# A message-passing layer on one core: the last split's loop re-ordered, one root for pair and finishing, filler products ahead of it

## The chip, the cores and the metric

The kernel runs on one core of one Trainium2 chip. The core has five engines with queues of their own: TensorE (PE in the profile; its weight loads are PEld), VectorE (DVE), ScalarE (ACT), GpSimd (POOL) and SyncE (SP, which here only starts transfers). They meet through semaphores. On-chip data lie in SBUF, and products land in the eight banks of PSUM. The metric is the device time of one execution, in microseconds (us); lower is better.

## The reference

```python
row, col = edge_index                                   # 100000 edges, 6250 nodes, D = 128
msg_in = concatenate([x[row], x[col], edge_attr], -1)   # 384 wide
h = msg_in @ W + b
mu, var = mean(h, -1), mean((h - mu)**2, -1)
h = (h - mu) * rsqrt(var + 1e-5) * gamma + beta
out = segment_sum(relu(h), row)                         # per source node
return layernorm(x + out)                               # no gain, no offset
```

Each edge takes a row of x for its source and one for its target, goes through one linear layer, a layer norm and a relu, and is summed into its source node. At the end each node is normalised once more.

## The kernel before

The linear layer is split by the three parts of its input. For the source part a table xa lies in SBUF, as three bf16 terms whose sum is the f32 value, for 50 blocks of 125 nodes. The target part and the edge part are computed edge by edge in the order in which the edges come (by target), and written to DRAM by an indirect transfer on POOL's queue (L561), sorted by block of the source. Each written row is 132 wide: 128 values and, in column D, the source's place in its block. The edges are worked off in six *splits*; each has its own sorted area, and while the products of one split are scattered, the blocks of the split before it are gathered and summed. The blocks are taken two at a time, as 25 *pairs* for each split.

What is done for one pair p of a split with k tiles of 128 edges a pair (k = 4 in the last split) are the methods of `Pair`:

- `load_pair` (L610): one transfer on SP's queue brings the pair's sorted rows into a tile hl (4 buffers).
- `ones` (L627): DVE compares column D with 0..127 and writes a one-hot, ohe, in f32 (4 buffers).
- `turn` and `turned` (L636, L647): PE transposes the one-hot into the bank tr (there is one), and ACT copies it out as bf16, ohn (2 buffers).
- `pick` (L656): PE adds, for each tile, the three terms of xa chosen by ohn onto hl. In the last split hl itself gets into the bank (of sel or hp) by a product with the identity, L665; in the other splits ACT copies it there (`seed`, L650).
- `square` (L675): ACT squares the k tiles with a running sum each (L680) and takes the root (L683).
- `root` and `scale` (L686, L691): DVE takes the reciprocal (L689), multiplies by it and cuts from below (L695), which gives msg (2 buffers).
- `sums` (L698): PE multiplies the one-hot with msg and sums over edges in the bank pa (there is one). `add` (L707): DVE adds pa to acc in SBUF (L712).

`Finish` does the last norm for the two blocks of a pair once the last split has been added: `begin` (L722) loads x for them on SP's queue and starts y on POOL (L728, L729; on DVE for the last pair); `stats` (L731) ends y and sums it on DVE; `root` (L740) squares on ACT (L745) and takes a root (L748); `norm` and `moved` (L750, L755) make the reciprocal (L753) and the shift (L758) on DVE; `end` (L761) multiplies and adds on POOL as two operations on 256 elements (L764, L765; by ACT, L768, for the last pair), and stores on SP's queue (L770).

PE, DVE, ACT and SP run in the order in which the program text issues the instructions; POOL's order is a scheduler's. Up to the last split, `work` (L876) issues the steps of all pairs of splits 0 to 4 from the table FLOW, in between the products of the edges. The last split has nothing of the edges beside it. Its order is `tail(i)` (L962), called once for each pair and six more times: it holds steps of pairs i+2 to i-1 and of finishings i-1 to i-5. Ahead of it, the last calls of `work` still issue steps of the last pairs of split 4, and `tail(-2)` and `tail(-1)` stand among them:

```python
    for p in range(2):
        load_pair(s, p)
    work(n_last - 8 - n_steps)
    tail(-2)
    work(n_last - 4 - n_steps)
    tail(-1)
    work(n_last - n_steps)
```

The first load of the last split waits for the last scatter of the edges to land, as its rows may be anywhere in the sorted area.

Of the kernel before, what the change touches and what calls it, by code (L numbers as in the profile page):

```python
# [8 lines left out]
F32 = mybir.dt.float32  # L9
# [7 lines left out]
P = 128  # L17
# [33 lines left out]
XG = 4  # L51
ROW = 132
# [29 lines left out]


def fast_path(ctx, tc, io, bad_d):
# [533 lines left out]
    class Pair:  # L618
# [8 lines left out]
        def ones(self):  # L627
# [4 lines left out]
            nc.vector.tensor_tensor(self.ohe[:, :k, :],  # L632
                                    self.hl[:, :k, D:D + 1].to_broadcast([P, k, P]),
                                    row_bc(iota_p, k), op=ALU.is_equal)
# [20 lines left out]

        def pick(self, g):  # L656


            j0, m = self.groups[g]
            if g in self.sel:  # L660
                sel = self.sel[g]
            else:
                name = "hp" if (g + self.p * len(self.groups)) % 2 else "sel"
                sel = psum.tile([P, PT, P], F32, name=name, bufs=BANKS[name])
                nc.tensor.matmul(sel[:, :m, :], ident, self.hl[:, j0:j0 + m, 0:D], start=True,  # L665
                                 stop=False, skip_group_check=True)
                self.sel[g] = sel
            for j in range(m):
                b = 2 * self.p + (j0 + j) % 2
                for i in range(3):  # L670
                    pe(nc.tensor.matmul(sel[:, j, :], self.ohn[:, j0 + j, :],  # L671
                                        xa[:, b, i * D:(i + 1) * D], start=False,
                                        stop=j == m - 1 and i == 2, skip_group_check=True))

# [41 lines left out]
    class Finish:  # L716
# [5 lines left out]
        def begin(self):  # L722
            fin, b0, n = late["fin"], self.b0, self.n
            xs = fin.tile([P, FN, D], F32, name="xs", bufs=3)
            nc.sync.dma_start(flat(xs), io["xblk"][:, b0 * D:(b0 + n) * D])
            self.y = fin.tile([P, FN, D], F32, name="y", bufs=6)
            engine = nc.gpsimd if b0 + n < NB else nc.vector
            engine.tensor_tensor(self.y, acc[:, b0:b0 + n, 0:D], row_bc(g2, n), op=ALU.mult)  # L728
            engine.tensor_tensor(self.y, self.y, xs, op=ALU.add)  # L729

        def stats(self):  # L731
            fin, y = late["fin"], self.y
            total = fin.tile([P, FN], F32, name="total", bufs=4)
            for j in range(self.n):
                nc.vector.scalar_tensor_tensor(y[:, j, :], beta_p, acc[:, self.b0 + j, D:D + 1],
                                               y[:, j, :], op0=ALU.mult, op1=ALU.add,
                                               accum_out=total[:, j:j + 1])
            self.total = total

        def root(self):  # L740
            fin = late["fin"]
            fsq = fin.tile([P, FN, D], F32, name="fsq")
            var = fin.tile([P, FN], F32, name="var")
            for j in range(self.n):
                nc.scalar.activation(fsq[:, j, :], self.y[:, j, :], AF.Square, scale=-float(D),  # L745
                                     bias=self.total[:, j:j + 1], accum_out=var[:, j:j + 1])
            self.std = fin.tile([P, FN], F32, name="fstd", bufs=3)
            nc.scalar.activation(self.std, var, AF.Sqrt, bias=eps, scale=1.0 / D ** 3)  # L748

        def norm(self):  # L750
            fin = late["fin"]
            self.rstd = fin.tile([P, FN], F32, name="frstd", bufs=3)
            nc.vector.reciprocal(self.rstd, self.std)  # L753

        def moved(self):  # L755
            fin = late["fin"]
            self.shift = fin.tile([P, FN], F32, name="shift", bufs=3)
            nc.vector.scalar_tensor_tensor(self.shift, self.total, -1.0 / D, self.rstd,  # L758
                                           op0=ALU.mult, op1=ALU.mult)

        def end(self):  # L761
            y, n = self.y, self.n
            if self.b0 + n < NB:
                nc.gpsimd.tensor_tensor(y, y, col_bc(self.rstd[:, :n], D), op=ALU.mult)  # L764
                nc.gpsimd.tensor_tensor(y, y, col_bc(self.shift[:, :n], D), op=ALU.add)  # L765
            else:
                for j in range(n):
                    nc.scalar.activation(y[:, j, :], y[:, j, :], AF.Identity,  # L768
                                         bias=self.shift[:, j:j + 1], scale=self.rstd[:, j:j + 1])
            nc.sync.dma_start(io["out"][:, self.b0 * D:(self.b0 + n) * D], flat(y))  # L770
# [183 lines left out]
    f = [Finish(2 * p, 2) for p in range(n)]  # L954

    def at(p):
        return 0 <= p < n

    first_g = range(len(x[0].groups) - 1)
    last_g = len(x[0].groups) - 1  # L960

    def tail(i):  # L962
        if at(i - 1):
            x[i - 1].root(last_g)
        if at(i + 2):
            x[i + 2].ones()
            if at(i + 4):
                load_pair(s, i + 4)
        if at(i - 1):
            x[i - 1].scale(last_g)  # L970
        if at(i):
            for g in first_g:
                x[i].pick(g)
                x[i].square(g)
            x[i].pick(last_g)
        if at(i - 4):
            f[i - 4].root()
        if at(i + 1):
            x[i + 1].turn()
            x[i + 1].turned()  # L980
        if at(i):
            x[i].square(last_g)
        if at(i - 5):
            f[i - 5].end()
        if at(i - 3):
            f[i - 3].stats()
        if at(i - 4):
            f[i - 4].norm()
        if at(i):
            for g in first_g:  # L990
                x[i].root(g)
        if at(i - 4):
            f[i - 4].moved()
        if at(i - 1):
            x[i - 1].sums()
        if at(i):
            for g in first_g:
                x[i].scale(g)
        if at(i - 1):
            x[i - 1].add()  # L1000
            f[i - 1].begin()


# [265 lines left out]
```

## Time and profile before

| | us |
|---|---|
| median of three runs | 1138.0 |
| lowest, highest | 1137.83, 1139.56 |
| the profiled execution | 1138.6 |
| its span, first to last instruction | 1136.7 |
| busy in the span: PE, DVE, POOL, ACT | 859.8, 882.7, 837.0, 735.6 |
| last scatter issued (start) | 1033.08 |
| first one-hot of the last split (start) | 1037.87 |
| last row of arithmetic (end) | 1129.76 |

The profile is of one execution. Its page gives busy times of the engines, the chain of work that ended last, and groups of instructions by line. The trace behind it can be asked for windows (busy time of each engine and the clock that TensorE was granted, as a share of full speed), for a timeline, and for the instructions of one line. Times in it count from the first instruction. A row of the timeline gives start, length, engine, line, operation, what it writes and reads, and in brackets how long its engine had been idle and what ended that.

POOL is 74% busy over the span, nearly all of it with the scatters, 782 of them at 986 ns each. The last split runs after the last of these, in the last tenth of the span.

### The profile page before, as it was taken

How to read it: one execution, taken by the hardware profiler on the slowest of the kernel's cores; microseconds unless marked ns; L12 is line 12 of the kernel's file. 1: busy time of each engine (PE TensorE's matmuls, PEld its weight loads, DVE VectorE, ACT ScalarE, POOL GpSimd, SP SyncE). 2: the span in 40 equal slices, each digit the busy share in tenths (PEclk: the TensorE clock that was granted, in tenths of full speed). 3: DMA queues.
4: the chain of work that ended last, by engine and by line, in shares of the span. 5: the costliest groups of instructions: out<-in, count | busy, mean ns of one | idle time of the engine just before them, and what ended most of it. 6: DMA issues, size and time to landing. Idle time of an engine off the chain costs nothing.

```text
span 1136.7 us, 27306 instructions
## 1 busy us (share of the span) xinstructions
PE 859.8 (76%) x8671; PEld 798.3 (70%) x8671; DVE 882.7 (78%) x2444; ACT 735.6 (65%) x3104; POOL 837.0 (74%) x899
## 2 busy tenths in 40 slices
PE   3657755445877878787778878898989899986994
PEld 2546644345877778686777877888988898975673
DVE  7987776326878777778677778988999987875996
ACT  1334332115666676576766777887988999994996
POOL 2777777777777777777777777777777777773786
PEclk9878786657989989899889999998999999998998
DMA  6799996438877756677777749776877677742562
GB/s 198 230 282 280 292 288 203 140 105 263 252 243 241 246 179 190 216 241 243 226 244 225 229 125 316 253 251 205 279 249 237 209 230 221 237 140 88 159 171 83
DMA packets 126674, 247.47 MB, mean 218 GB/s; under 512 B 47356, under 2 KB 61197, under 8 KB 126519
## 3 DMA queue, kind: packets, MB, share of 16 engines
q1 hardware_dynamic: 100356, 191.52, 56.2%
q0 software_dynamic: 25184, 53.31, 13.2%
q8 instruction: 70, 1.15, 0.4%
q10 hardware_dynamic: 978, 0.80, 0.3%
q14 instruction: 86, 0.70, 0.2%
HBM read 155.74 MB, written 89.80 MB: 216 GB/s over the span
## 4 chain that ended last, share of the span: by engine, by line
PE 29%; DMA 24%; DVE 24%; ACT 11%; issue 7%; POOL 2%; SPq 1%; ACTq 0%; POOLq 0%; DVEq 0%
DMA sorted<-hs,place_i 18%; PE pa L704 9%; DVE msg L695 7%; PE hp L531 7%; PE sel L671 6%; DMA db<-drel_d 4%; ACT sq L680 3%; DVE ohe L632 3%; DVE sc L391 3%; PE beside L428 2%; ACT sel L654 2%; POOL sorted L561 2%; ACT hs L543 2%; ACT ohn L648 2%; PE tr L644 2%
## 5 line engine op out<-in xcount | busy, mean ns | idle before, releaser
L561 POOL DMA_INDIRECT sorted<-hs,place_i x782 | 771.0, 986 | 240.9 <-issue 98.8
L704 PE MATMUL pa<-msg,ohe 128*128 128x130 f32 x1900 | 268.1, 292 | 23.3 <-DVE acc L712 15.3
L531 PE MATMUL hp<-w,eT 128*128 128x128 f32 x1564 | 248.2, 309 | 49.2 <-ACT hs L543 44.3
L543 ACT COPY hs<-hp 128x512 f32<-128x512 f32 x196 | 114.0, 582 | 258.7 <-DMA sorted<-hs,place_i 193.3
L671 PE MATMUL sel<-xa,ohn 128*128 128x128 bf16 x2706 | 198.7, 225 | 106.3 <-ACT sel L654 105.5
L671 PEld LDWEIGHTS <-ohn 128*128 128x128 bf16 x2850 | 182.9, 100 | 133.5 <-issue 112.6
L704 PEld LDWEIGHTS pa<-msg,ohe 128*128 128x128 f32 x1900 | 240.3, 201 | 34.3 <-DVE acc L712 18.7
L695 DVE SCALAR_TENSOR_TENSOR msg<-sel,rstd,cut 128x128 f32<-128x128 f32 x902 | 255.2, 345 | 8.0
L531 PEld LDWEIGHTS hp<-w,eT 128*128 128x128 f32 x1564 | 221.2, 218 | 54.6 <-ACT hs L543 48.8
L680 ACT ACTIVATE sq<-sel 128x128 f32<-128x128 f32 x902 | 238.1, 282 | 17.4 <-PE sel L671 16.7
L680 ACT ACTIVATION_READ_ACCUMULATOR sq<-sel 128x1 f32 x902 | 191.6, 212 | 0.0
L632 DVE TENSOR_TENSOR ohe<-hl,beside 128x1024 f32<-128x1024 f32 (+2 forms) x150 | 147.9, 986 | 37.4 <-DMA hl<-sorted 30.9
L654 ACT COPY sel<-hl 128x512 f32<-128x512 f32 (+1 forms) x225 | 127.9, 568 | 19.4 <-DVE msg L695 19.1
L648 ACT COPY ohn<-tr 128x1024 bf16<-128x1024 bf16 (+2 forms) x150 | 123.7, 825 | 18.4 <-PE tr L644 18.2
L689 DVE RECIPROCAL rstd<-std 128x4 f32<-128x4 f32 (+1 forms) x250 | 42.9, 172 | 84.7 <-ACT std L683 83.8
L519 DVE TENSOR_SCALAR ohd<-db,part_w 128x512 bf16<-128x512 bf16 x194 | 71.8, 370 | 46.7 <-DMA db<-drel_d 25.2
L644 PE MATMUL tr<-ident_h,ohe 128*128 128x128 bf16 x950 | 81.6, 226 | 10.5 <-issue 7.2
L535 PE MATMUL hp<-win,ohd 126*128 126x128 bf16 x782 | 83.3, 233 | 4.1 <-DVE ohd L519 3.5
L683 ACT ACTIVATE std<-ss,eps 128x4 f32<-128x4 f32 (+1 forms) x250 | 74.3, 297 | 8.1
L535 PEld LDWEIGHTS <-ohd 126*128 126x128 bf16 x782 | 66.9, 106 | 8.7 <-DVE ohd L519 3.7
L712 DVE TENSOR_TENSOR acc<-acc,pa 128x260 f32<-128x260 f32 x125 | 52.3, 418 | 26.4 <-PE pa L704 26.3
L644 PEld LDWEIGHTS <-ohe 128*128 128x128 bf16 x950 | 63.8, 102 | 11.8 <-issue 7.7
(159 smaller groups left out, 807.6 us busy)
## 6 DMA issues: line engine op xcount, KB each, us to landing
eT<-in_eT SPq DMA_DIRECT2D x96, 512.0 KB
hl<-sorted SPq DMA_DIRECT2D x75, 528.0 KB
db<-drel_d SPq DMA_DIRECT2D x96, 256.0 KB
sorted<-empty SPq DMA_DIRECT2D x100, 198.0 KB
hl<-sorted SPq DMA_DIRECT2D x50, 264.0 KB
sorted<-hs,place_i POOLq DMA_INDIRECT x782
hl<-sorted SPq DMA_DIRECT2D x25, 396.0 KB
sorted<-empty SPq DMA_DIRECT2D x50, 132.0 KB
```

The source lines that it names most:

```text
L531: pe(nc.tensor.matmul(hp[:, j, :], eT[:, at], w[:, 2, :], start=j == 0, stop=False, skip_group_check=True), 4)
L535: pe(nc.tensor.matmul(hp[:, j, :], oh[:3 * WN, at], win[:3 * WN, :], start=False, stop=j == m - 1, skip_group_check=True))
L543: nc.scalar.copy(hs[:, :m, 0:D], hp[:, :m, :])
L561: i = nc.gpsimd.indirect_dma_start(out=sorted_d[s][:, :], out_offset=bass.IndirectOffsetOnAxis(ap=place_i[:parts, t:t + 1], axis=0), in_=h ...
L632: nc.vector.tensor_tensor(self.ohe[:, :k, :], self.hl[:, :k, D:D + 1].to_broadcast([P, k, P]), row_bc(iota_p, k), op=ALU.is_equal)
L644: pe(nc.tensor.transpose(tr[:, j, :], half[:, j0 + j, 1::2], ident_h))
L648: nc.scalar.copy(self.ohn[:, :self.k, :], self.tr[:, :self.k, :])
L654: nc.scalar.copy(self.sel[g][:, :m, :], self.hl[:, j0:j0 + m, 0:D])
L671: pe(nc.tensor.matmul(sel[:, j, :], self.ohn[:, j0 + j, :], xa[:, b, i * D:(i + 1) * D], start=False, stop=j == m - 1 and i == 2, skip_gro ...
L680: nc.scalar.activation(sq[:, j, :], self.sel[g][:, j, :], AF.Square, accum_out=ss[:, j:j + 1])
L695: nc.vector.scalar_tensor_tensor(self.msg[:, j0 + j, 0:D], self.sel[g][:, j, :], rstd[:, j:j + 1], cut, op0=ALU.mult, op1=ALU.max)
L704: pe(nc.tensor.matmul(self.pa[:, h, :], self.ohe[:, j, :], self.msg[:, j, :], start=(j == h), stop=(j == k - 2 + h)), 4)
```

## The change

The steps of the last pairs of split 4 now all end before the first one-hot of the last split is issued. Four pairs are loaded ahead instead of two. Fourteen products of 128x512 ones, whose result nothing reads, are issued on PE between the old pairs' last sums and the new pairs' first product, all into the one bank tr. The order of `tail` is a new one, called for i from -1 to n+3. In it one tile of sums takes the squares of pair i (4 columns) and of finishing i-3 (2 columns), ACT takes one root of all six, and DVE one reciprocal; to fit the finishing's scale, the pair's squares are now of 128 times the value. The identity product of pair i+1 is issued a turn ahead (`begin_pick`), the sums of pair i-1 last in PE's turn. The add and the begin of the finishing move from one pair behind to two. x is loaded at i+1, three turns ahead of its use, into 5 buffers instead of 3. POOL ends a finishing by one fused multiply and add for each block, with scalars per partition; the last two are shared by ACT and DVE.

```diff
+WARM = 14
...
+        def begin_pick(self, by_pe):
+            m = self.k
+            name = "hp" if self.p % 2 else "sel"
+            sel = psum.tile([P, PT, P], F32, name=name, bufs=BANKS[name])
+            if by_pe:
+                nc.tensor.matmul(sel[:, :m, :], ident, self.hl[:, :m, 0:D], start=True,
+                                 stop=False, skip_group_check=True)
...
+        def squares(self, ss):
+            sq = late["blk"].tile([P, PT, P], F32, name="sq")
+            for j in range(self.k):
+                nc.scalar.activation(sq[:, j, :], self.sel[0][:, j, :], AF.Square,
+                                     scale=float(D), accum_out=ss[:, j:j + 1])
...
-            if self.b0 + n < NB:
-                nc.gpsimd.tensor_tensor(y, y, col_bc(self.rstd[:, :n], D), op=ALU.mult)
-                nc.gpsimd.tensor_tensor(y, y, col_bc(self.shift[:, :n], D), op=ALU.add)
...
+                    engine.tensor_scalar(y[:, j, :], y[:, j, :], self.rstd[:, j:j + 1],
+                                         self.shift[:, j:j + 1], op0=ALU.mult, op1=ALU.add)
...
+    def roots(i):
+        lo, hi = 0 if at(i) else kp, kp + FN if at(i - 3) else kp
+        if lo == hi:
+            return
+        std = late["blk"].tile([P, kp + FN], F32, name="tstd", bufs=2)
+        nc.scalar.activation(std[:, lo:hi], sums_of.pop(i)[:, lo:hi], AF.Sqrt, bias=eps,
+                             scale=1.0 / D ** 3)
+        rstd_of[i] = std, lo, hi
+
+    def reciprocals(i):
+        if i not in rstd_of:
+            return
+        std, lo, hi = rstd_of.pop(i)
+        rstd = late["blk"].tile([P, kp + FN], F32, name="trstd", bufs=4)
+        nc.vector.reciprocal(rstd[:, lo:hi], std[:, lo:hi])
+        if at(i):
+            x[i].rstd[0] = rstd
+        if at(i - 3):
+            f[i - 3].moved(rstd[:, kp:kp + FN])
 
     def tail(i):
+        if i == -1:
+            x[0].begin_pick(True)
+        if at(i):
+            x[i].pick(0)
+        if at(i + 1):
+            x[i + 1].turn()
+        reciprocals(i - 1)
+        if at(i - 2):
+            x[i - 2].add()
+            f[i - 2].begin(nc.gpsimd if i - 2 < n - 1 else nc.vector)
+        if at(i + 2):
+            ones_at(i + 2)
+            load_next()
+        if at(i - 1):
+            x[i - 1].scale(0)
+        if at(i + 1):
+            if i >= 0:
+                x[i + 1].begin_pick(True)
+            f[i + 1].load()
+        if at(i - 2):
+            f[i - 2].stats()
+        if at(i) or at(i - 3):
+            sums_of[i] = late["blk"].tile([P, kp + FN], F32, name="tsums", bufs=3)
+        if at(i - 3):
+            f[i - 3].square(sums_of[i][:, kp:])
+        if at(i):
+            x[i].squares(sums_of[i])
+        roots(i)
+        if at(i + 1):
+            x[i + 1].turned()
+        if at(i - 1):
+            x[i - 1].sums()
+        if at(i - 4):
+            f[i - 4].end([nc.gpsimd] if i - 4 < n - 2 else [nc.scalar, nc.vector])
+            f[i - 4].store()
...
-    for p in range(2):
-        load_pair(s, p)
-    work(n_last - 8 - n_steps)
-    tail(-2)
-    work(n_last - 4 - n_steps)
-    tail(-1)
-    work(n_last - n_steps)
+    for p in range(4):
+        load_next()
+    work(n_last + 1 - n_steps)
+    for p in range(WARM):
+        tr = psum.tile([P, PT, P], F32, name="tr", bufs=BANKS["tr"])
+        nc.tensor.matmul(flat(tr), ones_h, row_bc(ones_h, PT), start=True, stop=True)
     nc.vector.tensor_copy(beta_p, beta2)
-    for i in range(n + 6):
+    ones_at(0)
+    for i in range(-1, n + 4):
         tail(i)
```

The old `tail`, whose lines are left out of the diff, is printed above.

More of the change, by code (lines that the diff above doesn't have):

```diff
@@ L736, in stats, with square @@
                                                y[:, j, :], op0=ALU.mult, op1=ALU.add,
[L737 to L743, printed above, removed]
+                                               accum_out=self.total[:, j:j + 1])
+        def square(self, var):
+            fsq = late["fin"].tile([P, FN, D], F32, name="fsq")
             for j in range(self.n):
@@ L746, in root, with moved, end, store @@
                                      bias=self.total[:, j:j + 1], accum_out=var[:, j:j + 1])
[L747 to L758, printed above, removed]
+        def moved(self, rstd):
+            self.rstd = rstd
+            self.shift = late["fin"].tile([P, FN], F32, name="shift", bufs=3)
+            nc.vector.scalar_tensor_tensor(self.shift, self.total, -1.0 / D, rstd,
                                            op0=ALU.mult, op1=ALU.mult)
[L761 removed]
+        def end(self, engines):
             y, n = self.y, self.n
[L763 to L767 removed]
+            for j in range(n):
+                engine = engines[j % len(engines)]
+                if engine is nc.scalar:
                     nc.scalar.activation(y[:, j, :], y[:, j, :], AF.Identity,
                                          bias=self.shift[:, j:j + 1], scale=self.rstd[:, j:j + 1])
[L770 removed]
+                else:
+                    engine.tensor_scalar(y[:, j, :], y[:, j, :], self.rstd[:, j:j + 1],
+                                         self.shift[:, j:j + 1], op0=ALU.mult, op1=ALU.add)
+        def store(self):
+            nc.sync.dma_start(io["out"][:, self.b0 * D:(self.b0 + self.n) * D], flat(self.y))
     n_split = len(SPLITS)
```

90 lines of the change are left out of this document (34 added, 56 removed).

## Prediction

> **What bounds the kernel now.** I read the busy windows first, because the diff touches only the last split and the hand-over to it. The columns are the stretch, its length, then busy time (and instructions) of PE, PEld, DVE, ACT and POOL, the granted TensorE clock, the DMA share and GB/s.
>
> ```profile
> 1033.00:1033.50 0.50, 0.00 (x0) 0.00 (x0) 0.33 (x2) 0.00 (x0) 0.42 (x1) 0.88 0.37 127
> 1043.50:1044.00 0.50, 0.50 (x11) 0.50 (x9) 0.00 (x0) 0.00 (x0) 0.00 (x0) 0.88 0.00 0
> 1060.00:1080.00 20.00, 19.15 (x162) 14.17 (x163) 18.76 (x85) 18.73 (x97) 16.28 (x26) 1.00 0.63 170
> ```
>
> Two stages show. The two 0.88 rows are mixtures of 1.00 and 0.50, which puts a fall of the clock to half near 1033.4 and its rise near 1043.6. From 1060 on PE, DVE and ACT are each over 93% busy at full clock, so this stage is a loop among three full engines. The chain of waits (start, length, what) shows who holds whom, first across the hand-over, then over two pairs of the steady stage:
>
> ```profile
> 1035.24 2.61 DMA hl<-sorted
> 1037.87 0.69 DVE ohe L632
> 1038.56 0.35 DVE acc L712
> 1038.95 2.10 PE pa L704 x8
> ...
> 1057.05 0.59 ACT ohn L648
> ...
> 1059.22 0.57 DVE ohe L632
> 1059.79 0.27 DVE msg L695
> 1060.20 1.36 PE pa L704 x8
> 1061.56 0.86 PE sel L665 x2
> 1062.42 0.67 PE sel L671 x12
> 1063.09 0.24 PE tr L644 x4
> ```
>
> The hand-over waits for the first load of the last split until 1037.87. Only then, since L632 stands ahead of it on DVE, comes an old pair's add L712, which PE's old sums had been waiting for; and they run at half clock, 2.10 us against the 1.16 of the row at 1017.97 below. The first square of the last split starts at 1044.92. The second fence is one turn of 1063.35 - 1057.05 = 6.30 us for two pairs. Between the copy and the one-hots lie ACT's squares and root. In the turn PE alone gives 1.36 + 0.86 + 0.67 + 0.24 = 3.13 us a pair, with the sums paced by the scales, which come just ahead of them. From the timeline (start, length, engine, line):
>
> ```profile
> 1017.97 1.16 PE L704 MATMUL pa<-msg,ohe 128*128 128x130 f32 x8 [0.82 <-DVE acc L712]
> 1018.97 0.39 PE L644 MATMUL tr<-ident_h,ohe 128*128 128x128 bf16 x4
> 1019.19 0.83 PE L671 MATMUL sel<-xa,ohn 128*128 128x128 bf16 x12
> 1020.06 0.28 ACT L680 ACTIVATE sq<-sel 128x128 f32<-128x128 f32 x1
> 1021.24 0.30 ACT L683 ACTIVATE std<-ss,eps 128x4 f32<-128x4 f32 x1
> 1021.44 0.58 ACT L654 COPY sel<-hl 128x512 f32<-128x512 f32 x1
> 1044.44 0.59 ACT L648 COPY ohn<-tr 128x512 bf16<-128x512 bf16 x1 [2.34 <-PE tr L644]
> 1044.92 0.28 ACT L680 ACTIVATE sq<-sel 128x128 f32<-128x128 f32 x1
> 1045.15 0.83 PE L671 MATMUL hp<-xa,ohn 128*128 128x128 bf16 x12
> 1120.08 0.26 ACT L680 ACTIVATE sq<-sel 128x128 f32<-128x128 f32 x1
> 1128.88 0.88 ACT L768 ACTIVATE y<-y,shift,frstd 128x128 f32<-128x128 f32 x2 [0.71 <-DVE shift L758]
> ```
>
> So the 25 pairs take 1120.08 - 1044.92 = 75.16 us from first to last square (24 steps of 3.13), and the drain takes 1129.76 - 1120.08 = 9.68 us. These are the three terms of the sum: hand-over, step, drain. All before the hand-over stays as it is.
>
> **The change, part by part: the steady step.** One root and one reciprocal now serve a pair and the finishing three pairs behind it. That takes L748 from ACT and L753 from DVE; the squares of the finishing go ahead of those of the pair; the sums of pair i-1 go to the end of PE's turn, behind the next identity product (L665).
>
> ```profile
> L745 ACT ACTIVATE fsq<-y,total 128x128 f32<-128x128 f32 x50 | 19.3, 387 | 2.0 <-DVE y L735 2.0
> L748 ACT ACTIVATE fstd<-var,eps 128x2 f32<-128x2 f32 x25 | 7.4, 296 | 0.8
> L753 DVE RECIPROCAL frstd<-fstd 128x2 f32<-128x2 f32 x25 | 4.0, 160 | 0.9 <-ACT fstd L748 0.9
> L728 POOL TENSOR_TENSOR y<-acc,g 128x256 f32<-128x256 f32 x24 | 16.4, 685 | 18.9 <-DVE rstd L689 17.5 <-DVE acc L712 1.4
> L729 POOL TENSOR_TENSOR y<-y,xs 128x256 f32<-128x256 f32 x24 | 17.5, 728 | 5.3 <-DMA xs<-in_xblk 3.8
> L764 POOL TENSOR_TENSOR y<-y,frstd 128x256 f32<-128x256 f32 x24 | 14.7, 614 | 6.6 <-DVE frstd L753 6.4
> masks.py:199 POOL TENSOR_SCALAR_AFFINE_SELECT ident<-ident 128x128 f32<-128x128 f32 x1 | 0.3, 282 | 0.0
> ```
>
> What is then the longest loop? In after's order every ACT copy of a one-hot (ohn) releases its products, these the pair's squares, these the root, and the next copy stands behind the root. Its links, start to start: copy to products 1045.15 - 1044.44 = 0.71; products to squares 1020.06 - 1019.19 = 0.87; squares to root 1021.24 - 1020.06 = 1.18; root to the next copy 1021.44 - 1021.24 = 0.20. Sum 2.96 us, against 3.13 now. The engines' own queues must be shorter. ACT: copy 0.48 (1044.92 - 1044.44), finishing squares 2 x 0.39 = 0.78, then 1.18 and 0.20: 2.64. PE: 0.67 + 0.24 + 0.86, and sums no longer paced, 1.00 (1018.97 - 1017.97): 2.77. DVE: of its 18.76 us in 20, that is 2.93 a pair, 0.16 goes: 2.77. POOL: L728 and L729 1.41, plus two fused operations, plus about 0.08 between any two (1087.43 less 1086.74 + 0.61, below). The fused operation has no row. Its bounds are 0.28 (the one POOL operation of that shape with one tensor) and 0.61 (L764, two tensors and twice the elements); I take 0.33, nearer the first, as it has the same shape and one more scalar. POOL then needs 1.63 + 0.66 = 2.29. With 0.61 it needs 2.85, still under 2.96. The wait for xs (3.8 us in all on L729) goes too, but POOL is not on the path, so I count nothing; the cover is the 0.6 us by which POOL is shorter than the step.
>
> I take 2.96: 24 x 2.96 = 71.04, a gain of 4.12 us. Bounds: no gain, if PE stays the bound at 3.13; and 2.77, the longest queue, a gain of 8.7 us, which I hold for out of reach because the loop of links allows no overlap.
>
> The queues the steps pass: the hl load of pair i+5 now waits on SP for PE's identity product of pair i+1; behind it stand the xs load and the store of pair i-4. A load has three steps (8.9 us) to land where the first took 2.61, so this costs nothing. On DVE the finishing's sums (L735) wait for POOL's two operations on the add just made: 0.39 to reach the other engine (1038.95 - 1038.56), 1.41 and 0.08 give 1.88 us after the add's start, while add, one-hots and scales (1.13, the row at 1032.20 below) fill 0.35 + 0.57 + 1.13 = 2.05. That is tight: once POOL is late by more than this 0.17 and DVE's slack of 2.96 - 2.77 = 0.19 together, each further tenth costs 2.4 us over the split.
>
> DVE's shift (L758) is the other place where POOL reaches DVE:
>
> ```profile
> 1086.74 0.61 POOL L764 TENSOR_TENSOR y<-y,frstd 128x256 f32<-128x256 f32 x1 [0.38 <-DVE frstd L753]
> 1087.43 0.61 POOL L765 TENSOR_TENSOR y<-y,shift 128x256 f32<-128x256 f32 x1
> 1089.49 0.72 POOL L729 TENSOR_TENSOR y<-y,xs 128x256 f32<-128x256 f32 x1 [0.80 <-DMA xs<-in_xblk]
> 1089.72 0.51 DVE L758 SCALAR_TENSOR_TENSOR shift<-total,frstd 128x2 f32<-128x2 f32 x1
> ```
>
> The shift took 0.51 here and ended at 1090.23, when POOL's operation did. In the changed order it stands behind the joint reciprocal and may meet a fused operation, of 0.33 by my price, under the add's own wait for PE. I charge nothing. The Trainium skill (SBUF — State Buffer, Who interferes with whom) says that a VectorE instruction with two SBUF inputs is blocked for as long as a GpSimd instruction that reads SBUF runs. The trace agrees in this row, and the rule speaks against the change in that short POOL operations in a row leave the same total; by it the step would be up to 0.1 us longer, 2.4 us in all.
>
> **The hand-over.** The old adds go ahead of the first one-hots. The last scales end at 1033.33; an add follows them, and the sums 0.39 behind its start, as above:
>
> ```profile
> 1032.20 1.13 DVE L695 SCALAR_TENSOR_TENSOR msg<-sel,rstd,cut 128x128 f32<-128x128 f32 x4
> L588 PE MATMUL sel<-ones_h x3: 380/467/634, 217.0 to 217.7; 128*128 128x512 bf16 x3
> ```
>
> So the old sums start near 1033.72, long before the load lands. But the clock fell at 1033.4 from a history that does not change, so I let them run at half clock, 2.10 us, to 1035.82. Then come 14 added products of 128x512, all into the one bank of tr, each marked to wait for the one before. The fastest of the same shape takes 0.38, the slowest 0.63 (L588). I read these as full and half clock. With 0.04 for the wait (from a product's end, 1019.19 + 0.83, to the square behind it at 1020.06) that is 0.42 and 0.67. PE is busy from 1033.7, so I let the clock rise after a third of its 10.2 us at half, near 1036.8: two products at 0.67, twelve at 0.42, the next operation 0.22 behind the last start (0.67 / 12 x 4 of L671): 1035.82 + 1.34 + 11 x 0.42 + 0.22 = 1042.00. Then the identity product 0.86, transposes 0.39 and 0.04, and the links 0.71 and 0.87, together 2.87: first square at 1044.87, a gain of 0.05 us. Bounds: products that do not wait and a clock that never falls, 1033.72 + 1.16 + 14 x 0.22 + 2.87 = 1040.83, a gain of 4.1, and just behind the load's landing; all 14 at half clock, 1035.82 + 13 x 0.67 + 0.44 + 2.87 = 1047.84, a loss of 2.9. I take the middle because the row of L588 is the same product on banks that need no wait, and it shows no start under 0.35 apart ((217.7 - 217.0) / 2), so neither end is near. The Trainium skill (TensorE: Matmul & The Clock Gate, What's actually happening) states a free-running window of about 3.4 us for both changes of the clock; the 10.2 us between fall and rise here are three of these, so the trace agrees.
>
> **The drain.** Worked out as an estimate from the same links, from the last square: to the root 1.18, to the reciprocal 0.33, shift and add 0.5, scales 1.13, the last half of the sums 0.6, so 3.7 us. The last add then stands on DVE behind the finishing's sums of pair 23, for which POOL is 1.1 late (its two operations follow an add that itself came at 2.0). Then add 0.49, two operations on DVE 0.97, sums 0.66, squares 0.88, root 0.33, reciprocal and shift 0.41, the last rows shared by ACT and DVE 0.50: 4.2. Together 9.1 us against 9.68, a gain of 0.6. Were the 1.1 nothing, 1.7; were it doubled, a loss of 0.5.
>
> The sum: 0.05 + 4.12 + 0.6 = 4.8 us. The profiled execution took 1138.6 us (span 1136.7, the rest lies around it), 0.6 over the median of 1138.0. 1138.6 - 4.8 = 1133.8, or 1133.2 at the median's level, as all times below.
>
> **The rivals.** Bare products: the added products do not really wait, gain 4.1 + 4.12 + 0.6: 1129.2. For it: nothing reads tr in between; against: each is marked. Cold products: half clock through all 14, 2.9 lost, 4.7 won: 1136.2. For it: PE waits a third of each; against: sums keep it busy from 1033.7. The step does not shrink: PE stays at 3.13 as its 96% suggests, and only 0.6 is left: 1137.4; so the change would not do what it says. POOL becomes the bound: the fused operation reads two scalars per partition in a form without a row. From 0.77 each, POOL's pass of 1.63 + 2 x 0.77 = 3.17 eats the gains; at 0.9 it is 3.43, 24 x 3.43 - 75.16 = 7.2 lost, 0.6 won: 1144.6, slower. Against it: 0.28 for the nearest shape.
>
> **How the numbers follow.** Chances: the forecast 0.50 (1131 to 1135), bare products 0.17, step unchanged 0.13, cold products 0.08, POOL the bound 0.12. A measurement here tells 0.2%, about 2.3 us. Faster by more holds the forecast, bare products and 0.06 of the two weak cases: 0.73; within 0.2% the rest of these: 0.15; slower 0.12. The range 1128.5 to 1139.0 holds all but POOL's case and the far edge of the bare products.
>
> **What would show it.** Right: squares of successive pairs 2.96 apart; fused operations near 0.33; first square near 1044.9, last row near 1125; the sums at 1033.7 with PE at 0.50. Wrong: PE at over 95% in the split with the step still at 3.1; POOL without idle time; added products 0.22 apart; the first square after 1046.

## The result, and the profile after

| | before | after |
|---|---|---|
| median of seven runs, us | 1138.0 | 1142.59 |
| lowest, highest | 1137.08, 1139.56 | 1140.54, 1146.62 |
| the profiled execution | 1138.6 | 1146.62 |
| its span | 1136.7 | 1144.8 |
| ratio of the times, 95% interval | | 1.0047 [1.0031, 1.0062] |

The change made the kernel slower by 0.47%; 1133.2 us and "faster" were predicted. The profiled execution of after happens to be the slowest of its seven, so its 8.0 us over before are more than the 4.6 of the medians. The three terms of the prediction can be read off it, but for the profiled pair alone: they come to 7.4 us there, more than the medians differ by, and the executions without a profile can't be taken apart like this.

First the hand-over. From the timeline of after (start, length, engine, line, operation, what it writes and reads, how often, and in brackets the idle time before it and what ended that; rows of other work between them are left out, in the later fences too):

```profile
1035.94 2.10 PE L720 MATMUL pa<-msg,ohe 128*128 128x130 f32 x8 [1.21 <-DVE acc L728]
1036.44 9.05 SPq L615 DMA_DIRECT2D hl<-sorted  x5
1037.83 6.46 PE L1051 MATMUL tr<-ones_h 128*128 128x512 bf16 x14
1039.15 1.50 DVE L638 TENSOR_TENSOR ohe<-hl,beside 128x512 f32<-128x512 f32 x2 [0.44 <-DMA hl<-sorted]
1044.12 1.02 PE L667 MATMUL sel<-hl,ident 128*128 128x512 f32 x2
1046.92 0.28 ACT L688 ACTIVATE sq<-sel 128x128 f32<-128x128 f32 x1 [0.94 <-PE sel L681]
...
1127.36 0.25 ACT L688 ACTIVATE sq<-sel 128x128 f32<-128x128 f32 x1
...
1137.34 1.02 ACT L773 ACTIVATE y<-y,shift,trstd 128x128 f32<-128x128 f32 x2
```

The first load of the last split is issued at 1036.44, 1.2 us later than before (1035.24); that lies ahead of the change, as the last scatter already starts 1.2 us later (1034.28 against 1033.08). Its rows have landed when the one-hots start at 1039.15. The product that needs only them, L667, starts at 1044.12, because the 14 added products stand ahead of it on PE. From the issue of the load to the first square it takes 1046.92 - 1036.44 = 10.48 us, where before took 9.68: 0.8 lost.

Then the step: 1127.36 - 1046.92 = 80.44 us from the first to the last square, 5.28 more than before. And the drain: 1138.36 - 1127.36 = 11.00 us against 9.68, 1.3 lost. The four differences, 1.2 + 0.8 + 5.28 + 1.3 = 8.6 us, are the time by which the last row of arithmetic ends later (1138.36 against 1129.76).

So most of the loss is the steps. Squares of successive pairs are 2.88 us apart at first (1046.92, 1049.80, 1052.68, 1055.55, 1058.43), and 3.47 from 1061.40 on, when the finishings have set in. Which engine is full there? The windows of after (busy time and instructions of PE, PEld, DVE, ACT, POOL, then clock, DMA share, GB/s):

```profile
1060.00:1080.00 20.00, 18.41 (x153) 12.58 (x153) 16.72 (x71) 15.72 (x84) 12.76 (x24) 1.00 0.53 162
```

None is. PE, DVE and ACT have 1.6, 3.3 and 4.3 us idle in 20, and POOL, the engine that the prediction kept for a rival, is the least busy of the four at 64%. Where no engine is full and the step is longer, the profile is to be read for a loop of waits. The groups of 1060 to 1120 (count, busy time, mean of one in ns, idle time just before, and what ended it) give its corners:

```profile
L776 POOL TENSOR_SCALAR y<-y,trstd,shift 128x128 f32<-128x128 f32 x34 | 14.9, 448 | 19.4 <-DVE shift L765 19.4
L759 ACT ACTIVATE fsq<-y,total 128x128 f32<-128x128 f32 x35 | 13.8, 395 | 13.3 <-DVE y L752 13.3
L752 DVE SCALAR_TENSOR_TENSOR y<-beside,acc,y 128x128 f32<-128x128 f32 x36 | 11.2, 349 | 10.3 <-POOL y L746 10.3
L765 DVE SCALAR_TENSOR_TENSOR shift<-total,trstd 128x2 f32<-128x2 f32 x17 | 2.7, 161 | 0.6
```

Nearly all of POOL's idle time ends with DVE's shift, and DVE's idle time ends with POOL. Two engines that wait for each other once in every step are a loop. The timeline shows one turn of it:

```profile
1078.68 0.88 POOL L776 TENSOR_SCALAR y<-y,trstd,shift 128x128 f32<-128x128 f32 x2 [1.14 <-DVE shift L765]
1079.52 0.68 POOL L745 TENSOR_TENSOR y<-acc,g 128x256 f32<-128x256 f32 x1
1080.29 0.73 POOL L746 TENSOR_TENSOR y<-y,xs 128x256 f32<-128x256 f32 x1
1081.05 0.35 DVE L752 SCALAR_TENSOR_TENSOR y<-beside,acc,y 128x128 f32<-128x128 f32 x1 [0.57 <-POOL y L746]
1081.32 0.35 DVE L752 SCALAR_TENSOR_TENSOR y<-beside,acc,y 128x128 f32<-128x128 f32 x1
1081.59 0.19 DVE L990 RECIPROCAL trstd<-tstd 128x6 f32<-128x6 f32 x1
1081.82 0.16 DVE L765 SCALAR_TENSOR_TENSOR shift<-total,trstd 128x2 f32<-128x2 f32 x1
1082.16 0.45 POOL L776 TENSOR_SCALAR y<-y,trstd,shift 128x128 f32<-128x128 f32 x1 [1.14 <-DVE shift L765]
```

The two fused operations end finishing i-4. The next one's begin (L745, L746) stands behind them on POOL, though its add was made 1.1 us earlier (started at 1078.42). DVE's finishing sums (L752) wait for the begin, the reciprocal and the shift stand behind the sums on DVE, and the next fused operations wait for the shift. Start to start: 0.84 + 0.77 + 0.76 + 0.54 + 0.23 + 0.34 = 3.48 us, the step.

The program text has the begin ahead of the end in each turn. But POOL's order is not the text's: the scheduler put the end of i-4 ahead of the begin of i-2. The links show that these operations go round, but not that their order is what makes the step long; nor do they show what the added products are worth. That was tried.

### The profile page after: what moved, and what is told of

Its sections match the earlier page's. It is cut to its first block, busy times and chain, and to the rows that moved or that the text cites. A ratio compares the mean times of both kernels' runs of the same rounds, so it can differ in the third digit from the quotient of the medians.

```text
span 1144.8 us, 27292 instructions
## 1 busy us (share of the span) xinstructions
PE 869.2 (76%) x8685; PEld 800.6 (70%) x8685; DVE 879.9 (77%) x2424; ACT 727.8 (64%) x3082; POOL 828.9 (72%) x897
## 5 line engine op out<-in xcount | busy, mean ns | idle before, releaser
L720 PE MATMUL pa<-msg,ohe 128*128 128x130 f32 x1900 | 272.0, 295 | 21.8 <-DVE msg L711 11.5
L532 PE MATMUL hp<-w,eT 128*128 128x128 f32 x1564 | 244.4, 306 | 50.2 <-ACT hs L544 45.5
L720 PEld LDWEIGHTS pa<-msg,ohe 128*128 128x128 f32 x1900 | 245.1, 204 | 47.2 <-DVE acc L728 13.5
L532 PEld LDWEIGHTS hp<-w,eT 128*128 128x128 f32 x1564 | 217.9, 215 | 55.8 <-ACT hs L544 50.5
L711 DVE SCALAR_TENSOR_TENSOR msg<-sel,rstd,cut 128x128 f32<-128x128 f32 x850 | 240.7, 345 | 8.0
L696 ACT ACTIVATE sq<-sel 128x128 f32<-128x128 f32 x850 | 223.6, 281 | 20.7 <-PE sel L681 20.3
L696 ACT ACTIVATION_READ_ACCUMULATOR sq<-sel 128x1 f32 x850 | 180.2, 212 | 0.0
L705 DVE RECIPROCAL rstd<-std 128x4 f32<-128x4 f32 (+1 forms) x225 | 38.6, 172 | 78.2 <-ACT std L699 77.5
L699 ACT ACTIVATE std<-ss,eps 128x4 f32<-128x4 f32 (+1 forms) x225 | 66.9, 297 | 7.3
```

Source lines behind the costliest of these rows:

```text
L532: pe(nc.tensor.matmul(hp[:, j, :], eT[:, at], w[:, 2, :], start=j == 0, stop=False, skip_group_check=True), 4)
L696: nc.scalar.activation(sq[:, j, :], self.sel[g][:, j, :], AF.Square, accum_out=ss[:, j:j + 1])
L711: nc.vector.scalar_tensor_tensor(self.msg[:, j0 + j, 0:D], self.sel[g][:, j, :], rstd[:, j:j + 1], cut, op0=ALU.mult, op1=ALU.max)
L720: pe(nc.tensor.matmul(self.pa[:, h, :], self.ohe[:, j, :], self.msg[:, j, :], start=(j == h), stop=(j == k - 2 + h)), 4)
```

## The experiments

The theory: (1) POOL's order closes a loop of 3.47 us, and the other order opens it; (2) the added products stand in the way of the first new product and cost more than their clock brings. The rivals: POOL's own work, or its hold on DVE, sets the step whatever the order; the fused form itself is the trouble; the products pay for themselves.

The chips of these runs were slower through the earlier splits, where before took 1367.3, 1349.5 and 1349.1 us, so each ratio is to the before of the same chip, and differences between kernels are read from the last split, whose operations take the same time there.

**POOL's order alone.** The fused operations of i-4 are made to follow the begin of i-2:

```diff
-            engine.tensor_tensor(self.y, self.y, self.xs, op=ALU.add)
+            self.begun = engine.tensor_tensor(self.y, self.y, self.xs, op=ALU.add)
...
+                    if behind is not None and engine is nc.gpsimd:
+                        tc.add_manual_dep(i.ins, behind.ins.name, written, reason="end behind begin")
```

> After, with one order added on POOL: the two fused operations that end a finishing pair (L776) stand behind the begin of the later pair (L745, L746) in each step, as the text has them. Nothing is computed in another way. Theory (a loop of waits: shift, two fused operations, begin, finishing sums, root, shift): the loop is open, the finishing sums start some 0.9 us earlier, and a step goes from 3.47 to 2.9-3.1 us, so that the first to the last square is 70-74 us instead of 80.44 and the drain falls by up to 1.3 us: 1131 to 1135 us in all. Rival A (POOL's own work or its blocking of the other engines sets the step, the order on it does not): the step stays at 3.4-3.5 us and the time within 0.2% of after, about 1142. Rival B (the order only moves the wait, now to the outputs that leave later): step 3.2-3.4 us, 1137 to 1140.

Ratio to before 0.9984 [0.9969, 0.9999]. Steps are 2.88 us from the first to the last. From its timeline, the first and last square and one turn between them:

```profile
1277.38 0.28 ACT L688 ACTIVATE sq<-sel 128x128 f32<-128x128 f32 x1 [0.94 <-PE sel L681]
...
1314.12 0.41 DVE L728 TENSOR_TENSOR acc<-acc,pa 128x260 f32<-128x260 f32 x1
1314.62 0.69 POOL L745 TENSOR_TENSOR y<-acc,g 128x256 f32<-128x256 f32 x1 [0.43 <-DVE acc L728]
1315.38 0.73 POOL L746 TENSOR_TENSOR y<-y,xs 128x256 f32<-128x256 f32 x1
1316.14 0.35 DVE L752 SCALAR_TENSOR_TENSOR y<-beside,acc,y 128x128 f32<-128x128 f32 x1
1316.21 0.88 POOL L776 TENSOR_SCALAR y<-y,trstd,shift 128x128 f32<-128x128 f32 x2
1316.91 0.18 DVE L765 SCALAR_TENSOR_TENSOR shift<-total,trstd 128x2 f32<-128x2 f32 x1
1317.02 0.41 DVE L728 TENSOR_TENSOR acc<-acc,pa 128x260 f32<-128x260 f32 x1
1317.51 0.68 POOL L745 TENSOR_TENSOR y<-acc,g 128x256 f32<-128x256 f32 x1 [0.42 <-DVE acc L728]
...
1346.54 0.28 ACT L688 ACTIVATE sq<-sel 128x128 f32<-128x128 f32 x1 [0.16 <-PE sel L681]
```

POOL's begin now waits for the add and for nothing else, and L752 has no idle time ahead of it. First to last square takes 1346.54 - 1277.38 = 69.16 us, 11.28 less than after and 6.0 less than before; the drain takes 9.38. The same instructions with one order changed: part (1) is shown, and this run's rivals A and B fall. What sets the step now? The windows of the second to fourth step, when the finishings have hardly begun, and of the full loop:

```profile
1280.26:1288.90 8.64, 8.62 (x82) 6.61 (x80) 7.04 (x28) 7.28 (x39) 3.17 (x5) 1.00 0.45 145
1300.00:1340.00 40.00, 40.00 (x361) 31.27 (x359) 39.55 (x167) 37.30 (x195) 31.79 (x56) 1.00 0.59 184
```

DVE is busy 39.55 us of 40 in the full loop. But the step is 2.88 in the first window too, where DVE has 1.6 us idle in 8.64. What both share is the loop through ACT and PE that the prediction named: copy, products (by the load of their weights), squares, root, next copy.

```profile
1284.51 0.57 ACT L654 COPY ohn<-tr 128x512 bf16<-128x512 bf16 x1
1285.13 0.67 PEld L681 LDWEIGHTS <-ohn 128*128 128x128 bf16 x12 [0.20 <-ACT ohn L654]
1286.02 0.28 ACT L688 ACTIVATE sq<-hp 128x128 f32<-128x128 f32 x1 [0.16 <-PE hp L681]
1287.19 0.30 ACT L983 ACTIVATE tstd<-tsums,eps 128x6 f32<-128x6 f32 x1
1287.40 0.56 ACT L654 COPY ohn<-tr 128x512 bf16<-128x512 bf16 x1
```

Start to start it takes 0.62 + 0.89 + 1.17 + 0.21 = 2.89 us, the whole step. PE counts as busy throughout, but its weight loads wait for the copy. So this loop gives 2.88 by itself, and it takes 2.89 in the full loop too (copies at 1316.19 and 1319.08). DVE's queue, and the links add, begin, sums, shift, add (0.50 + 0.76 + 0.76 + 0.77 + 0.11 = 2.90), just fit beside it. The total fell short of the 1131 to 1135 expected, taken in proportion. In this execution the hand-over was longer, 16.60 us from the load's issue (1260.78) to the first square, against 10.48 in after:

```profile
1262.84 2.10 PE L720 MATMUL pa<-msg,ohe 128*128 128x130 f32 x8 [0.52 <-DVE acc L728]
1264.73 8.96 PE L1054 MATMUL tr<-ones_h 128*128 128x512 bf16 x14
1273.48 1.91 PE L667 MATMUL sel<-hl,ident 128*128 128x512 f32 x2
```

Here the clock had fallen ahead of the old sums and stayed at 0.50 through all 14 products, 0.64 us apart.

**No added products.** All else as in after:

```diff
-WARM = 14
+WARM = 0
```

> After without the 14 products that are added behind the old pairs' sums (their result is read by nothing). Theory (they are in the way: each waits for the one ahead, 0.43 us apart at full clock, and the first new product stands behind them): the first square comes 7.0 to 8.5 us after the load's issue instead of 10.48, even with the new products at half the clock, and the step stays at 3.47: -2 to -3.5 us, 1139 to 1140.5. Rival (the clock that they keep up is worth what they take): the first square at 10 us or later, or the same time with a longer first step: 1142 to 1145.

Ratio 1.0044 [1.0026, 1.0062]. By the time that is what the rival had (1142 to 1145 in proportion), and the first square came 8.78 us after the load's issue (1269.87), just past the 7.0 to 8.5 of the theory. The trace tells more than the total: on the same chip the hand-over from the last old sums to the first square took 6.40 us (1272.25 to 1278.65) against 14.54 with the products and POOL's order mended (1262.84 to 1277.38), both at half clock; POOL's order does not reach the hand-over, as no finishing runs there. First to last square took 80.88, the first step 3.16 instead of 2.88 at the half clock. So 8.1 us of products at half clock buy 0.3 back.

**After, once more, and with both repairs.** On one chip:

> The changed kernel once more, on the chip on which the next three run, so that they have it beside them. Theory: first to last square 80.4 us at steps of 3.47, and against before +4.6 us on a chip where the load of the new split is awaited, up to +13 where the clock falls ahead of the added products (then they take 0.64 each, 9 us in all). Rival (the loss of the first measurement belonged to that chip): within 0.2% of before.

> After with both repairs: the fused operations stand behind the later begin on POOL, and the 14 products are left out. Theory: steps of 2.88 as with the order alone (69.2 us from the first to the last square, 6.0 less than before) and the first square 4.0-4.5 us after the last old pair's add instead of 9 to 12: 5 to 8 us below before, 0.9930 to 0.9957 of it. Rival (the products' clock is worth something once the step is short): the first steps run at half the clock for 10 us and give 2-3 us back: 0.9975 or more.

After came to 1.0072 [1.0047, 1.0098] of before, with 80.42 us from first to last square (1257.30 to 1337.72). With POOL's order mended and the products left out, the ratio is 0.9921 [0.9891, 0.9951], 69.15 us: 1338.05 against 1349.52 of before and 1358.22 of after. It beats both, by slightly more than expected (0.9930 to 0.9957). The clock stayed at 1.00 in both hand-overs here. After's, and then the one without products:

```profile
1247.65 1.16 PE L720 MATMUL pa<-msg,ohe 128*128 128x130 f32 x8 [1.79 <-DVE acc L728]
1248.65 6.01 PE L1051 MATMUL tr<-ones_h 128*128 128x512 bf16 x14
1254.49 1.02 PE L667 MATMUL sel<-hl,ident 128*128 128x512 f32 x2
1257.30 0.28 ACT L688 ACTIVATE sq<-sel 128x128 f32<-128x128 f32 x1 [0.94 <-PE sel L681]
```

```profile
1243.42 1.16 PE L720 MATMUL pa<-msg,ohe 128*128 128x130 f32 x8 [0.98 <-DVE acc L728]
1244.53 1.10 PE L667 MATMUL sel<-hl,ident 128*128 128x512 f32 x2
1247.99 0.28 ACT L688 ACTIVATE sq<-sel 128x128 f32<-128x128 f32 x1 [0.94 <-PE sel L681]
```

9.65 us against 4.57 from the last old sums to the first square: the products cost 5.1 us at full clock. Of the 20.2 us between the medians of the two kernels, 11.3 are thus steps, 1.6 drain (10.98 against 9.39) and 5.1 products, 18.0 in all. The profiled executions are 22.2 us apart, and the other 4.2 of these lie ahead of the last old sums (1247.65 against 1243.42). Part (2) is shown, and without the products nothing was lost in the first steps, which are 2.87 and 2.88.

**Products in a gap.** Four of them ahead of the old split's last sums but one, where PE waits, and none behind:

```diff
-    work(n_last + 1 - n_steps)
+    work(4 * len(pairs) + 11 - n_steps)
     for p in range(WARM):
...
+    work(n_last + 1 - n_steps)
```

> As the last, with 4 such products in another place: ahead of the old split's last two message sums, in the 2.1 us in which TensorE waits for the messages, where they delay nothing if they take 4 x 0.43 us. Theory A (the clock falls because of the idle time there): the clock stays at 1.00 through the hand-over, each old sum takes 1.15 instead of 2.10 us and the first products 1.08 instead of 1.91: 2 to 3 us less than without them. Theory B (1.7 us of work is not enough, or the fall comes from earlier): clock 0.50 at the hand-over and the time within 0.2% of the kernel without them.

Ratio 0.9932 [0.9911, 0.9953], no gain. Theory A could not be tried, as the clock stayed at 1.00 with and without them. They had a price of another kind:

```profile
1242.26 0.28 ACT L696 ACTIVATE sq<-sel 128x128 f32<-128x128 f32 x1 [1.34 <-PE tr L1054]
```

The old pair's squares began 1.54 us after its picks (1240.72) where 0.87 is usual (1239.32 to 1240.19 without the products): by the profile an added product is what released ACT, so even in a gap they delayed the path by 0.67.

**Fused or not, in after's order.** `end` on POOL is again two operations over 256:

```diff
+            if engines == [nc.gpsimd]:
+                nc.gpsimd.tensor_tensor(y, y, col_bc(self.rstd, D), op=ALU.mult)
+                nc.gpsimd.tensor_tensor(y, y, col_bc(self.shift, D), op=ALU.add)
+                return
```

> After, with each finishing pair on POOL ended by two operations over 256 values as in before, in place of two fused ones over 128; POOL's order stays that of after. Theory (POOL's end lies in series in the loop of waits): two of some 0.61-0.65 us for two of 0.44 make the step longer by what they add, 0.35-0.45 us: 3.8-3.9 us a step, +8 to +10 us, 1150 to 1153 us. Rival A (the fused form is what disturbs, by its two operands for each partition): the step falls back to 3.1-3.3 us, 1133 to 1139. Rival B (POOL's end is not in the loop): no change, 1142 within 0.2%.

Ratio 1.0118 [1.0093, 1.0142], slower as the loop has it; but steps of 3.60 us, not 3.8 to 3.9. The first of the two needs only the reciprocal, not the shift, so it starts 0.27 us behind the reciprocal where the fused one starts 0.57 behind it (1082.16 - 1081.59). That takes back 0.30 of the 0.42 by which two operations are longer. The loop holds; the expectation had left that link out.

**Fused or not, in the mended order.** The last edit, with the fused operations' order of the first experiment put on L771, and the 14 products kept:

> The order on POOL repaired (14 products kept), and the pair ended by two operations over 256 instead of two fused ones over 128: what the fusing itself is worth once the order is right. Theory (the loop is open, so what is left of POOL is its queue: 0.68 + 0.73 + 0.61 + 0.61 with some 0.08 between them, 2.95 us): step 2.9-3.0 instead of 2.88, +0.5 to +3 us against the order alone. Rival A (VectorE's queue, 39.55 of 40 us, sets 2.88 and POOL has room): no change within 0.2%. Rival B (the fusing was the gain): back to 3.1 or more, +5 us.

Ratio 1.0034 [1.0011, 1.0057], steps of 3.30 us: rival B. The surprise is why. From the timeline:

```profile
1297.67 0.61 POOL L774 TENSOR_TENSOR y<-y,shift 128x256 f32<-128x256 f32 x1
1297.71 0.59 DVE L765 SCALAR_TENSOR_TENSOR shift<-total,trstd 128x2 f32<-128x2 f32 x1
1298.22 0.41 DVE L728 TENSOR_TENSOR acc<-acc,pa 128x260 f32<-128x260 f32 x1
```

```profile
L765 DVE SCALAR_TENSOR_TENSOR shift<-total,trstd 128x2 f32<-128x2 f32 x16 | 9.5, 596 | 0.6
```

The shift, two columns wide, takes 596 ns on the mean where it took 161 in after (POOL idle just then) and 184 in the fused kernel. It ends when POOL's L774 does. The add stands behind it on DVE, POOL's begin behind the add: the 0.41 by which it grew is the 0.42 of the step. The Trainium skill (SBUF — State Buffer, Who interferes with whom) says that a VectorE instruction with two SBUF inputs contends with a GpSimd instruction that reads SBUF, and one with at most one such input, outside certain fast modes, does not. If so, the cure is to read one tensor less:

```diff
-            nc.vector.scalar_tensor_tensor(self.shift, self.total, -1.0 / D, rstd,
-                                           op0=ALU.mult, op1=ALU.mult)
+            for j in range(self.n):
+                nc.vector.tensor_scalar(self.shift[:, j:j + 1], self.total[:, j:j + 1],
+                                        rstd[:, j:j + 1], -1.0 / D, op0=ALU.mult, op1=ALU.mult)
```

> The unfused pair with the order on POOL repaired (steps of 3.30 us, VectorE's shift L765 0.60 in each, ending with POOL's L774), with the shift made in another way: for each of the two columns one operation with one tensor (the totals) and two scalars, in place of one operation with two tensors from SBUF. The product is the same up to rounding. Theory (the shift is held up by POOL because it reads two tensors): the two take 0.15-0.2 us each, together 0.3-0.35 instead of 0.60, and the step is 3.0-3.1 us, -4.5 to -7 us against the unfused kernel. Rival A (VectorE is held up whatever it reads, while POOL's L774 runs): the first of the two takes 0.6 and the step is 3.3-3.5. Rival B (the loop over POOL is the bound, the shift stands beside it): 3.30.

```profile
1302.38 0.61 POOL L775 TENSOR_TENSOR y<-y,shift 128x256 f32<-128x256 f32 x1
1302.41 0.34 DVE L766 TENSOR_SCALAR shift<-total,trstd 128x1 f32<-128x1 f32 x2
1302.66 0.41 DVE L728 TENSOR_TENSOR acc<-acc,pa 128x260 f32<-128x260 f32 x1
```

Ratio 0.9981 [0.9957, 1.0005], steps of 3.04, 71.87 us from the first to the last square against 76.56. The pair of operations starts under POOL's L775 and is done in 0.34, well ahead of its end; the 0.16 by which it is longer than the 184 ns of the fused kernel is the 0.16 by which the step is longer than 2.88. The theory holds, and the trace agrees with the rule of the Trainium skill. The edit changed the kind of operation too, but L752 is of the old kind: it reads y from SBUF and its other tensor from PSUM, and takes 349 ns on the mean in after, in the mended order and in both unfused kernels, under POOL's operations or not.

**Fused operations alone, in before.**

```diff
-                nc.gpsimd.tensor_tensor(y, y, col_bc(self.rstd[:, :n], D), op=ALU.mult)
-                nc.gpsimd.tensor_tensor(y, y, col_bc(self.shift[:, :n], D), op=ALU.add)
+                for j in range(n):
+                    nc.gpsimd.tensor_scalar(y[:, j, :], y[:, j, :], self.rstd[:, j:j + 1],
+                                            self.shift[:, j:j + 1], op0=ALU.mult, op1=ALU.add)
```

> Before, with one part of the change alone: a pair is ended by two fused operations over 128 in place of two over 256; roots, order at the hand-over and POOL's order are those of before. Theory (the shift of before, 0.22 on the mean and 0.51 in some steps, is no longer held up, and little else hangs on POOL): the step falls from 3.15 to 3.05-3.13, -0.5 to -2.5 us, within 0.2% of before. Rival A (POOL's end is in a loop here too): 2.9-3.0, -4 us or more, 0.997 or less. Rival B (POOL's order puts the fused pair in the way as in the changed kernel): 3.2 or more, slower.

Ratio 0.9989 [0.9971, 1.0006], 1329.82 - 1254.89 = 74.93 us from the first to the last square (75.16 in before): nothing that a measurement tells. So fusing is worth nothing in before's order, and 7.4 us of steps in the mended one (76.56 against 69.16).

**The old pairs' steps ended ahead, alone, in before:**

```diff
-    work(n_last - 8 - n_steps)
-    tail(-2)
-    work(n_last - 4 - n_steps)
-    tail(-1)
...
+    tail(-2)
+    tail(-1)
```

> Before, with one part of the change alone: the old pairs' last two steps end ahead of the new split's first one-hots, with nothing added behind them; the rest of the last split is that of before (finishing and pairs with a root each, POOL's two operations over 256). Theory (the order at the hand-over is worth something by itself where nothing is put behind it): the first square moves from 9.68 us after the load's issue to 7.5-9 us, the step stays at 3.1, 1135.8 to 1137.5 us. Rival A (the old steps' end was hidden behind the load already): the same as before, 1138 within 0.2%. Rival B (the clock falls in the gap that they leave, and the new products pay for it): first square at 10 us or later, 1138.5 to 1140.

Ratio 1.0000 [0.9982, 1.0019]: rival A by the time. The first square came 8.19 us after the last old sums (1267.53 to 1275.72), at half clock, and 10.85 after the load's issue (1264.87), where rival B had 10 or more. Since before has no profile on that chip, whether something was won there and lost to the clock stays open.

## Why the prediction was wrong

**The step: wrong in sign, and this is the step that failed.** The prediction let "POOL's two operations on the add just made" start when the add is made, "1.88 us after the add's start", against 2.05 of fill. Ahead of them stood the two fused operations, 0.84 us of POOL start to start, and these had to wait for the shift first. "That is tight: once POOL is late by more than this 0.17 and DVE's slack ... together" named the very place; what it did not ask is which operation stands ahead of the begin on POOL, whose order the program text does not set. So -4.12 became +5.28. With only that order changed it is -6.0.

**"The cover is the 0.6 us by which POOL is shorter than the step".** POOL's 36% idle covered nothing, as each idle stretch ended with the shift: free time on an engine inside a loop is no cover. For the same reason the rival "POOL becomes the bound" came near the measured time by another road than its own. It needed 0.77 us for each fused operation; that took 0.448, within the bounds of 0.28 to 0.61 and above the 0.33 taken.

**The loop of links through ACT and PE, 2.96 us.** Right to within a tenth: it sets the step of 2.88 wherever POOL's loop doesn't, in the first steps of after, and in all of them once POOL's order is mended and the end stays fused. DVE is nearer to it than was thought: its queue was put at 2.77 and needs some 2.85 (39.55 / 40 x 2.88).

**"I charge nothing" for the shift under POOL.** Right for the fused form (184 ns). With the end left as two operations it was 0.42 us a step once the finishings had set in, 7.4 us in all (76.56 against 69.16). That "short POOL operations in a row leave the same total" was wrong: the fused two take 0.88 us where the others take 1.30, so they are done about when the shift comes. The contention spoke for the fusing, not against it.

**The hand-over.** The prices were right: 0.42 and 0.67 between products were predicted, 0.43 and 0.64 measured. From the load's issue to the first square 9.63 us were predicted and 10.48 measured, mostly because the old sums started 2.2 us later than put (1035.94 against 1033.72), of which 1.2 lie ahead. The clock's fall, taken as settled by what ran before, did not come at all in the hand-over on the chip of the two repairs. But the term was read only against before's 9.68, and the products were taken as part of the change that had to be paid. Set against the same kernel without them they are a plain loss of 5.1 us at full clock and 8.1 at half. "Bare products", the rival with 0.17, falls: each waits for the one ahead.

**The drain.** 9.1 was predicted, 11.00 measured, 9.38 with POOL's order mended (and 11.00 again there with the end unfused). The same failed step: the fused operations stand ahead of the last begins.

## What to carry to other kernels

For every engine whose order a scheduler sets, list what stands ahead of the instruction that the path waits for, and follow the waits until they close: a loop through two engines that both have time to spare (here 64% and 84% busy) can be longer than any queue. In the groups it shows as two engines whose idle time is ended by each other, each with time to spare. Filler work that keeps a clock up is to be priced against the same kernel without it, at both clocks, and from the moment the data have landed.

## What the runs showed of the hardware

The granted clock went to 0.50 at the hand-over for 3.4, 10.2 and 13.6 us in these three executions (after, 1035.7 to 1039.1; without products, 1271.0 to 1281.2; POOL's order alone, 1262.1 to 1275.7), once, three and four times 3.4 us, and not at all on the chip of the two repairs. In the longest of these the products kept PE busy nearly throughout:

```profile
1266.00:1268.00 2.00, 1.77 (x5) 0.33 (x4) 1.52 (x3) 0.00 (x0) 0.00 (x0) 0.50 0.00 0
...
1272.00:1274.00 2.00, 1.89 (x4) 0.73 (x3) 0.00 (x0) 0.00 (x0) 0.00 (x0) 0.50 0.00 0
```

PE counts 1.77 to 1.89 us busy of 2 from 1266 to 1274, yet the clock stays at half for 11.0 us from the first of the products (1264.73). The Trainium skill (TensorE: Matmul & The Clock Gate, What's actually happening) puts the warming at one window of some 3.4 us of sustained work; the trace does not agree here, as the products, 0.64 us apart and each waiting for the one ahead, did not raise the clock in 11.0 us, nor in 10.9 in the unfused kernel of after's order (1268.9 to 1279.9). Whether the short waits between them are the reason no run shows, nor why the clock was back 1.3 us after the first product in after (1037.83 to 1039.1).
